# Convolution diagonals of a second Mamba block made early and kept in DRAM, spare TensorE products at the start, and two blocks of softplus sums on GpSimd

## The chip, the cores and the metric

The kernel runs on one core of one Trainium2 chip, in one launch. The metric is the device time of an execution in microseconds (us). The engines are called as in the profile: PE is TensorE (PEld its weight loads), DVE is VectorE, ACT is ScalarE, POOL is GpSimd, SP is SyncE, whose queue only issues DMAs.

## The reference, cut to what matters

The network has four layers. The change touches the first alone, a group normalization of the input (2 images, 256 channels, 32 x 32 pixels) followed by two Mamba blocks:

```
def mamba_block(x, ...):                      # x: 2 x 1024 tokens x 256 channels
    xs, res = split(u @ in_w + in_b)          # 512 channels each
    xs = silu(depthwise_conv4(xs, conv_w) + conv_b)
    dt, Bm, Cm = split(xs @ xproj_w)          # 16, 16 and 16 columns
    delta = softplus(dt @ dt_w + dt_b)
    dA  = exp(delta * -exp(A_log))            # 16 states for each channel
    dBu = delta * Bm * xs
    h_t = dA_t * h_(t-1) + dBu_t              # a scan over the tokens of an image
    y   = sum_n(h * Cm) + xs * D
    return (y * silu(res)) @ out_w + out_b

xt = xt + layernorm(mamba_block(xt, m1...))
xt = flip(xt); xt = xt + layernorm(mamba_block(xt, m2...)); xt = flip(xt)
```

Behind it come an attention over shifted pixels, a linear attention with a mixture of experts, and a softmax attention with a second mixture of experts. All is in float32.

## The kernel before

Channels lie on the 128 partitions, in four blocks (`dc` = 0 to 3) of the 512 inner channels; tokens lie along the free dimension, in chunks of 512. There are four chunks, two to an image, so that layer 0 has eight units: block m1 with chunks 0 to 3, then m2 with chunks 0 to 3. Each chunk goes through four generators of class `Mamba`.

- `enter` (L337) projects the chunk (`in_w`) into `pre`, which has three more columns ahead for the convolution; they are set to zero on POOL for an image's first chunk and copied from the chunk before otherwise.
- `front` (L360) makes all that the scan needs. The convolution of length 4 is four TensorE products per block with diagonal weights `taps[:, dc * 4 + k, :]` (L383): 128 x 128 matrices that hold 128 convolution weights on their diagonal. Then come the silu, the product with `xproj_w` (L405), which gives `xd`, and the softplus. The latter is computed as max(v, 0) + ln(1 + exp(-|v|)): `project` takes the absolute value (L446) and the positive part (L448 or L450), `powers` takes the exponential and the logarithm and w (L455 to L464), and `sums` (L467) makes four additions and products out of these, the last of which is `du` = delta * xs.
- `scan` (L498) is the scan of one unit. For each of the 16 states n it loads row n of B for all partitions (`m_b`, SP queue, four buffers), multiplies `du` with it in two halves of 128 x 1024 (`m_h<-m_du,m_b`, six buffers), lets ACT make exp(delta * A) for each block (L569) and DVE scan along 512 tokens (L573): 64 scans a unit. `rest` turns the states to token-major on PE (L527, L529) and weighs them with C, on ACT for five states and on DVE for the others (L543).
- `back` (L593) gates, projects out, normalizes and adds. It takes the term xs * D as a TensorE product with four further diagonals, `skip` (L632).

The first chunk has no scan of another to lie beside, and so has a `front` of its own (`alone=True`): its convolution runs on PE for blocks 0 and 2 and as four tap steps each on DVE for blocks 1 and 3 (L370, L375); DVE takes the positive part (L448) and w (L460) of all four blocks; the four sums of each block are on DVE; and DVE multiplies both halves of the first state (L557).

The order of the work is set in four ways. Layer 0 is laid out by `layer0` (L718): `paced` (L695) spreads the steps of the next chunk's `front` and of the last chunk's `back` over the 63 slots between the scans of a unit, by the slots given in `steps`. POOL's instructions go through `net.lined` (L174), which holds each one behind the one before it in the program. `tc.issue_after(i)` holds an instruction behind i. Beyond that the framework plans the order on each engine when it compiles, and the trace shows places where it isn't that of the source: some products of the second image's normalization (L248) stand between those of the first chunk's projection (L353).

The lines that matter for the change are these. `GroupNorm.image` (L238) normalizes one image: statistics on DVE, two small products on PE (L248, L257), the root on ACT (L159, L160) and four steps on DVE (L263). `diagonals` (L305) makes the 16 matrices of `taps` on POOL, each as identity times a column. It is called at once for m1, and for m2 at L784, as 16 steps over slots 24 to 40 of unit 2. `load_rest` (L316) loads the gate's and the output's weights and makes the four `skip` matrices on POOL, for m1 at once, for m2 in unit 4, the second part at slot 62. `load` (L292) makes `aneg` = -exp(A_log), on ACT (L301) and DVE (L302). Each of `taps` and `skip` has one buffer, which m2 takes over from m1. `delta` and `du` have two buffers each.

Of the kernel before, what the change touches and what calls it, by code (L numbers as in the profile page):

```python
# [10 lines left out]
F32 = mybir.dt.float32  # L11
# [8 lines left out]
P = 128  # L20
# [7 lines left out]
TC = 512  # L28
# [3 lines left out]
NDC = DI // P  # L32
# [186 lines left out]
class GroupNorm:  # L219
# [3 lines left out]
    def __init__(self, net, pool, psum, x):  # L223
# [12 lines left out]
        )  # L236

    def image(self, b):  # L238
        net, nc, pool, x = self.net, self.net.nc, self.pool, self.x
        n = NCC  # L240
        mv = pool.tile([P, n, 2], F32, name=f"gn_mv{b}")
        for cc in range(NCC):
            st = net.small.tile([P, 2, 6], F32, tag="gn_st", name=f"gn_st{b}{cc}")
            for h in range(2):
                nc.vector.bn_stats(out=st[:, h, :], in_=x[:, cc, b, h * 512 : (h + 1) * 512])
            nc.vector.bn_aggr(out=mv[:, cc, :], in_=st.rearrange("p h s -> p (h s)"))
        ps = self.psum.tile([P, TC], F32, tag="ht", name=f"gn_ps{b}")
        nc.tensor.matmul(ps[:, :n], lhsT=self.grp, rhs=mv[:, :, 0], start=True, stop=True)  # L248
        gm = pool.tile([P, n], F32, name=f"gn_gm{b}")
        nc.vector.tensor_copy(gm, ps[:, :n])  # L250

        d = pool.tile([P, n], F32, name=f"gn_d{b}")
        nc.vector.tensor_sub(d, mv[:, :, 0], gm)
        nc.vector.tensor_mul(d, d, d)
        nc.vector.tensor_add(d, d, mv[:, :, 1])
        ps = self.psum.tile([P, TC], F32, tag="ht", name=f"gn_ps2{b}")
        nc.tensor.matmul(ps[:, :n], lhsT=self.grp, rhs=d, start=True, stop=True)  # L257
        rs = pool.tile([P, n], F32, name=f"gn_rs{b}")
        net.rstd(rs, ps[:, :n])
        for h in range(2):  # L260
            for cc in range(NCC):
                xh = x[:, cc, b, h * TC : (h + 1) * TC]
                nc.vector.tensor_scalar(  # L263
                    xh, xh, gm[:, cc : cc + 1], rs[:, cc : cc + 1], ALU.subtract, ALU.mult
                )


class Mamba:
# [11 lines left out]
    def __init__(self, net, m, pools, xt, x, in_w, out_w, xproj_w, dt_w):  # L280
        self.net, self.m, self.xt, self.x = net, m, xt, x
        self.wpool, self.one, self.two, self.scanp, self.dram, self.ps_mm, self.ps_da, self.ps_ht = pools
        self.weights = in_w, out_w, xproj_w, dt_w
        self.chunks = {}
        self.due, self.pre = {}, {}

# [17 lines left out]

    def diagonals(self):  # L305

        self.taps = self.wpool.tile(
            [P, NDC * 4, P], F32, tag="taps", name=f"{self.m}_taps"
        )
        for i in range(NDC * 4):  # L310
            self.net.lined(
                self.net.nc.gpsimd.tensor_scalar_mul, self.taps[:, i, :], self.net.ident, self.net.col(f"{self.m}_conv_w", i)
            )
            yield

    def load_rest(self):  # L316

        net, nc, m, wpool = self.net, self.net.nc, self.m, self.wpool
        in_w, out_w, xproj_w, dt_w = self.weights
        self.gate_sb = wpool.tile([P, NCC, DI], F32, tag="gate_w", name=f"{m}_gate_sb")  # L320
        nc.sync.dma_start(self.gate_sb, in_w[:, :, DI:])
        yield
        self.out_sb = wpool.tile([P, NDC, C], F32, tag="out_w", name=f"{m}_out_sb")
        nc.sync.dma_start(self.out_sb, out_w)

        self.skip = wpool.tile([P, NDC, P], F32, tag="skip", name=f"{m}_skip")
        for dc in range(NDC):
            net.lined(
                nc.gpsimd.tensor_scalar_mul, self.skip[:, dc, :], net.ident, net.col(f"{m}_D", dc)
            )  # L330
        yield
# [4 lines left out]

    def enter(self, j):  # L337

        net, nc, m, one = self.net, self.net.nc, self.m, self.one
        tok = slice(j * TC, (j + 1) * TC)  # L340
        if not self.first(j):
            carry = self.wpool.tile([P, NDC, 3], F32, tag="carry", name=f"{m}_carry_{j}", bufs=2)
            net.lined(nc.gpsimd.tensor_copy, carry, self.entered[:, :, TC : TC + 3])
        self.entered = pre = one.tile([P, NDC, 3 + TC], F32, tag="pre", name=f"{m}_pre_{j}")
        self.pre[j] = pre
        if self.first(j):
            net.lined(nc.gpsimd.memset, pre[:, :, 0:3], 0.0)
        else:
            net.lined(nc.gpsimd.tensor_copy, pre[:, :, 0:3], carry)
        for mc in range(NDC):  # L350
            ps = self.ps_mm.tile([P, TC], F32, tag="mm", name=f"{m}_in_{j}_{mc}")
            for kc in range(NCC):
                nc.tensor.matmul(  # L353
                    ps, lhsT=self.in_sb[:, kc, mc * P : (mc + 1) * P], rhs=self.xt[:, kc, tok],
                    start=(kc == 0), stop=(kc == NCC - 1),
                )
            nc.scalar.activation(pre[:, mc, 3:], ps, AF.Identity, bias=net.col(f"{m}_in_b", mc))
            yield

    def front(self, j, alone=False):  # L360

        net, nc, m, one, two = self.net, self.net.nc, self.m, self.one, self.two
        eng = nc.vector if alone else nc.gpsimd
        pre = self.pre.pop(j)
        xs = two.tile([P, NDC, TC], F32, tag="xs", name=f"{m}_xs_{j}", bufs=3)
        silus = []
        for dc in range(NDC):
            b = net.col(f"{m}_conv_b", dc)
            if alone and dc % 2:
# [4 lines left out]
                for k in range(1, 4):  # L374
                    nc.vector.scalar_tensor_tensor(  # L375
                        xs[:, dc, :], pre[:, dc, k : k + TC],
                        net.col(f"{m}_conv_w", dc * 4 + k), xs[:, dc, :], ALU.mult, ALU.add,
                    )
# [58 lines left out]
        def project(eb, a):  # L437
            for k, dc in enumerate(range(a.start, a.stop)):
# [7 lines left out]
                nc.scalar.activation(eb[:, k, :], ps, AF.Abs, bias=b)  # L446
                if alone:
                    nc.vector.tensor_scalar(delta[:, dc, :], ps, b, 0.0, ALU.add, ALU.max)  # L448
# [17 lines left out]

        def sums(eb, lb, w, a):  # L467
            d = delta[:, a, :]
# [10 lines left out]
        if alone:  # L479
            for a in parts:  # L480
                w = du[:, a, :]
                yield from project(e[:, a], a)
                yield from powers(e[:, a], ln[:, a], w)
                yield from sums(e[:, a], ln[:, a], w, a)
        else:
# [12 lines left out]
    def scan(self, j, before, between, start=False, last=False):  # L498
# [50 lines left out]
        for n in range(NS):  # L549
# [3 lines left out]
            for g in range(NDC // G):  # L553
                h = scanp.tile(half, F32, tag="h", name=f"{m}_h_{j}_{n}_{g}", bufs=6)
                factors = du[:, g * G : (g + 1) * G, :], b.unsqueeze(1).to_broadcast(half)
                if start and n == 0:
                    nc.vector.tensor_mul(h, *factors)  # L557
# [160 lines left out]
def layer0(net, x, x_dram, m1, m2, load_image, taps, conv_dram, lg):  # L718
# [5 lines left out]
    with (  # L724
# [17 lines left out]
        blocks[0].load()  # L742
        for _ in blocks[0].diagonals():
            pass
        load_image()
# [3 lines left out]
        for m, r in zip(blocks, rows):  # L749
            m.out_b = r  # L750
        norm.image(0)

        units = [(m, j) for m in blocks for j in range(NCH)]
        norm.image(1)
        for _ in chain(units[0][0].enter(0), units[0][0].front(0, alone=True)):
            pass
        before, done, late = iter(()), [], []
        aside = taps.make(ps_mm, conv_dram)
        for u, (m, j) in enumerate(units):
# [1489 lines left out]
```

## Time and profile before

| | us |
|---|---|
| median of 3 runs | 2053.76 (2052.34 to 2054.6) |
| the profiled execution | 2042.13 |
| its span, first to last instruction | 2040.4 |
| layer 0 before its first scan | 50.5 |
| units 0 to 7, first scan to first scan | 113.4, 115.4, 122.7, 117.5, 119.6, 115.9, 119.4, 137.5 |
| busy in the whole span: PE, DVE, ACT, POOL | 1863.5, 1336.7, 947.2, 1062.2 |

How to read the profile: a line of a timeline has the start in us from the beginning of the span, the length in us, the engine (a q behind it is the engine's queue, which only issues), the line of the kernel, the operation, what is written and what is read, the shapes and the number of instructions merged into the line; in brackets behind it stand the idle time of the engine before it and who ended that. A line of a table of stretches has the stretch, its length, busy time and number of instructions for each engine, the granted share of the TensorE clock, and the share and rate of the DMA engines. L179 is the line of the helper `lined`, under which all of POOL's instructions of layer 0 appear; they are told apart by what they write. `m_taps` and `m_skip` are diagonals, `m_h` the products of `du` and B, `m_du`, `m_e` and `m_delta` the sums of the softplus.

### The profile page before, as it was taken

The page shows a single profiled execution, that of the slowest core. Times are in us where ns is not written, and L with a number is a line of the kernel's source. Part 1 is how long each engine was busy: PE and PEld are TensorE (multiplying, and loading weights), DVE is VectorE, ACT ScalarE, POOL GpSimd, SP SyncE. Part 2 cuts the span into 40 slices and gives each one's busy share as a digit, 9 for nine tenths or more (in the row PEclk, how much of TensorE's full clock was granted, in tenths as well). Part 3 has the DMA queues.
Part 4 walks back from the last instruction along what each step waited for, and adds up shares of the span by engine and source line. Part 5 has one row for each costly group of instructions (what it writes and reads, how often), then busy time and mean ns, then how long its engine had stood idle before and what let it go on. Part 6 is the DMA issues. An engine that isn't in the chain of part 4 may idle for free. (4 is left out here: it accounts for less than half of the span.)

```text
span 2040.4 us, 27838 instructions
## 1 busy us (share of the span) xinstructions
PE 1863.5 (91%) x9924; PEld 1336.6 (66%) x9924; DVE 1336.7 (66%) x2145; ACT 947.2 (46%) x1712; POOL 1062.2 (52%) x721
## 2 busy tenths in 40 slices
PE   7888987988898888899999989999999899999995
PEld 3465664656555565655566555568999666799994
DVE  6889899899988988898614285774222445652223
ACT  4787876777877777774302253332111122221111
POOL 3788898988979798994504260012333200023331
PEclk9789998999999999899999999999999999999997
DMA  3334354253435434362130100056999400358995
GB/s 125 98 91 118 86 123 107 70 132 85 128 90 117 108 76 123 78 146 67 31 58 1 52 0 1 24 196 247 322 324 324 183 21 21 142 179 319 329 333 201
DMA packets 98344, 269.15 MB, mean 132 GB/s; under 512 B 35851, under 2 KB 54160, under 8 KB 82068
## 3 DMA queue, kind: packets, MB, share of 16 engines
q1 hardware_dynamic: 80980, 196.72, 29.2%
q0 software_dynamic: 14208, 67.00, 13.5%
q10 hardware_dynamic: 3008, 3.55, 0.5%
q8 instruction: 83, 1.36, 0.3%
q14 instruction: 65, 0.53, 0.1%
HBM read 199.48 MB, written 21.46 MB: 108 GB/s over the span
## 5 line engine op out<-in xcount | busy, mean ns | idle before, releaser
L179 POOL TENSOR_TENSOR m_h<-m_du,m_b 128x1024 f32<-128x1024 f32 x254 | 604.6, 2470 | 160.0 <-PE m_ht L529 61.2
L569 ACT ACTIVATE m_da<-m_delta,m_aneg 128x512 f32<-128x512 f32 x512 | 349.6, 694 | 153.7 <-DVE m_h L573 150.7
L573 DVE TENSOR_TENSOR_SCAN m_h<-m_da,m_state,m_h 128x512 f32<-128x512 f32 x256 | 314.4, 1268 | 24.7 <-POOL m_h L179 15.1
L529 PEld LDWEIGHTS m_ht<-ident,m_h 128*128 128x128 f32 x1600 | 195.5, 148 | 198.1 <-issue 70.0
L529 PE MATMUL m_ht<-ident,m_h 128*128 128x128 f32 x1600 | 259.0, 289 | 60.8 <-DVE m_ya L543 30.1
L573 DVE TENSOR_TENSOR_SCAN m_h<-m_da,m_h 128x512 f32<-128x512 f32 x256 | 299.9, 1208 | 18.5 <-ACT m_da L569 11.7
L543 DVE SCALAR_TENSOR_TENSOR m_ya<-m_ht,m_ct,m_ya 128x512 f32<-128x512 f32 x324 | 231.9, 735 | 59.2 <-PE m_ht L529 53.1
L2008 PEld LDWEIGHTS h<-xts,we_l_late 128*128 128x128 f32 x2048 | 238.3, 192 | 9.1 <-issue 4.3
L2008 PE MATMUL h<-xts,we_l_late 128*128 128x128 f32 x2048 | 239.7, 275 | 4.4 <-DMA we_l_late<-in_l_experts_dram 2.9
L2016 DVE TENSOR_TENSOR hid<-hid,h 128x512 f32<-128x512 f32 x79 | 54.3, 687 | 233.9 <-PE h L2008 229.9
L1747 POOL DMA_INDIRECT x_l_early<-l_zs,l_source x15 | 17.4, 1158 | 340.5 <-ACT pt L1511 138.3
L2015 ACT ACTIVATE hid<-h 128x512 f32<-128x512 f32 x79 | 47.2, 597 | 315.4 <-issue 241.0
L527 PE MATMUL m_ht<-ident,m_h 128*128 128x128 f32 x896 | 137.0, 299 | 26.6 <-ACT m_s L541 9.4
L527 PEld LDWEIGHTS m_ht<-ident,m_h 128*128 128x128 f32 x896 | 120.1, 205 | 50.7 <-DVE m_h L573 17.6
L1747 POOL DMA_INDIRECT x_l_late<-l_zd,source x64 | 65.5, 1024 | 147.4 <-PE xt L1991 144.4
L2023 PE MATMUL o<-we_l_late,hid 128*128 128x256 f32 x512 | 122.7, 381 | 4.1 <-DVE y L2028 2.8
L383 PE MATMUL m_conv<-m_pre,m_taps 128*128 128x512 f32 x240 | 119.1, 615 | 4.1 <-ACT m_xs L389 4.1
L2030 POOL DMA_INDIRECT l_yd<-y,target x64 | 65.5, 1023 | 104.5 <-DVE y L2028 92.1
L541 ACT ACTIVATE m_s<-m_ht,m_ct 128x512 f32<-128x512 f32 x156 | 104.5, 686 | 27.8 <-PE m_ht L527 12.0
L2023 PEld LDWEIGHTS o<-we_l_late,hid 128*128 128x128 f32 x512 | 91.8, 190 | 15.3 <-DVE y L2028 3.9
L942 PE MATMUL early_acc<-x,early 128*98 128x448 f32 (+24 forms) x308 | 98.6, 446 | 0.4 <-DVE lg L959 0.4
L942 PE MATMUL acc<-x,pair 128*98 128x416 f32 (+21 forms) x308 | 93.3, 450 | 0.0
(399 smaller groups left out, 3104.3 us busy)
## 6 DMA issues: line engine op xcount, KB each, us to landing
we_l_late<-in_l_experts_dram SPq DMA_DIRECT2D x64, 1536.0 KB
m_yb<-m_s POOLq DMA_DIRECT2D x39, 1024.0 KB
m_b<-m_bd SPq DMA_DIRECT2D x128, 256.0 KB
we_l_early<-in_l_experts_dram SPq DMA_DIRECT2D x15, 1536.0 KB
m_ya<-m_yb POOLq DMA_DIRECT2D x7, 1024.0 KB
w<-in_l_w_dram SPq DMA_DIRECT2D x21, 256.0 KB
l_yl<-l_yd SPq DMA_DIRECT2D x8, 512.0 KB
l_zd<-l_z SPq DMA_DIRECT2D x7, 512.0 KB
```

Source lines behind the costliest of these rows:

```text
L179: self.line = do(*args, **named)
L383: nc.tensor.matmul(ps, lhsT=self.taps[:, dc * 4 + k, :], rhs=pre[:, dc, k : k + TC], start=(k == 0), stop=(k == 3),)
L527: nc.tensor.matmul(a, lhsT=h, rhs=net.ident, start=True, stop=True)
L529: nc.tensor.transpose(a, h, net.ident)
L541: nc.scalar.activation(to[:, i, :], ps, AF.Copy, scale=c)
L543: nc.vector.scalar_tensor_tensor(ya[:, i, :], ps, c, ya[:, i, :], ALU.mult, ALU.add)
L569: net.decayed = nc.scalar.activation(da, delta[:, dc, :], AF.Exp, scale=self.aneg[:, i : i + 1])
L573: nc.vector.tensor_tensor_scan(h, da, h, 0.0 if first else state[:, n, dc : dc + 1], ALU.mult, ALU.add)
L942: nc.tensor.matmul(a[:, lo - 16 * k : hi - 16 * k, co : co + n], lhsT=lhsT, rhs=self.x[:, kc, b, lo - r0 : hi - r0, ci : ci + n], start=(u ...
L1747: nc.gpsimd.indirect_dma_start(out=x, out_offset=None, in_=rows[:, :], in_offset=bass.IndirectOffsetOnAxis(ap=source[:, g : g + 1], axis=0 ...
L2008: nc.tensor.matmul(ps[:, at], lhsT=w12[:, s, kc, at], rhs=xt[:, kc * P : (kc + 1) * P], start=(kc == 0), stop=(kc == NCC - 1),)
L2023: gate.o = nc.tensor.matmul(ps[:, :C], lhsT=ht[:, mc * P : (mc + 1) * P], rhs=w[:, 8 + mc, :], start=(mc == 0), stop=(mc == NHC - 1),)
```

## The change

- **The diagonals of m2.** `keep_diagonals` makes all 20 of them on POOL right behind the first chunk's projection in the program, in buffers borrowed from the pools of `delta` and `du`, and writes them to DRAM by two DMAs from POOL's queue. The steps on POOL in unit 2 are gone; at slot 34 of that unit one DMA on SP fetches the 16 matrices of `taps` into their buffer. `load_rest` of m2 fetches `skip` in the same way.
- **Spare products.** `warm` issues products on PE whose result nobody reads: two of 512 columns ahead of the first image's first small product, two of 128 columns behind it, and three of 128 columns behind the second small product.
- **The second image's normalization** is cut in two. The first part, with the statistics and the small products, is held behind the first image's last normalization step and the third block's projection of the first chunk; the second part, with the root and the four steps on the image, behind the last tap step on DVE and the return of the exponential's table on ACT.
- **The first chunk.** The zero columns of `pre` are set on DVE. The positive part of block 3 goes from DVE to ACT. The sums of blocks 2 and 3 go from DVE to POOL (outside of `lined`). DVE multiplies three halves of states, not two: both of the first state and one of the second.

```diff
+    def warm(self, rows, n, *after):
+        net = self.net
+        ps = self.psum.tile([P, TC], F32, tag="ht", name="warm")
+        with ExitStack() as order:
+            for i in after:
+                order.enter_context(net.tc.issue_after(i.ins))
+            for _ in range(n):
+                net.nc.tensor.matmul(
+                    ps[:, : rows.shape[1]], lhsT=net.ident, rhs=rows, start=True, stop=True
+                )
...
+        if b == 0:
+            self.warm(x[:, 0, b, :TC], 2)
         ps = self.psum.tile([P, TC], F32, tag="ht", name=f"gn_ps{b}")
-        nc.tensor.matmul(ps[:, :n], lhsT=self.grp, rhs=mv[:, :, 0], start=True, stop=True)
+        last = nc.tensor.matmul(ps[:, :n], lhsT=self.grp, rhs=mv[:, :, 0], start=True, stop=True)
+        if b == 0:
+            self.warm(net.ident, 2, last)
...
+        last = nc.tensor.matmul(ps[:, :n], lhsT=self.grp, rhs=d, start=True, stop=True)
+        if b == 0:
+            self.warm(net.ident, 3, last)
+        yield
         rs = pool.tile([P, n], F32, name=f"gn_rs{b}")
         net.rstd(rs, ps[:, :n])
...
+    def scaled(self, out, name):
+        for i in range(out.shape[1]):
+            self.net.lined(
+                self.net.nc.gpsimd.tensor_scalar_mul, out[:, i, :], self.net.ident, self.net.col(name, i)
+            )
...
+    def keep_diagonals(self):
+        net, nc, m = self.net, self.net.nc, self.m
+        self.kept = []
+        for tag, name, n in (("delta", f"{m}_conv_w", NDC * 4), ("du", f"{m}_D", NDC)):
+            room = self.two.tile([P, NDC * 4, P], F32, tag=tag, name=f"{name}_room")[:, :n, :]
+            self.scaled(room, name)
+            kept = self.dram.tile([P, n, P], F32, tag=f"kept_{tag}", name=f"{name}_kept", bufs=1)
+            net.lined(nc.gpsimd.dma_start, kept, room)
+            self.kept.append(kept)
+
+    def fetch_diagonals(self):
+        self.net.nc.sync.dma_start(self.taps_tile(), self.kept[0])
+        yield
...
-        self.skip = wpool.tile([P, NDC, P], F32, tag="skip", name=f"{m}_skip")
-        for dc in range(NDC):
-            net.lined(
-                nc.gpsimd.tensor_scalar_mul, self.skip[:, dc, :], net.ident, net.col(f"{m}_D", dc)
-            )
+        if self.kept:
+            nc.sync.dma_start(self.skip_tile(), self.kept[1])
+        else:
+            self.scaled(self.skip_tile(), f"{m}_D")
         yield
...
-        if self.first(j):
+        if alone:
+            nc.vector.memset(pre[:, :, 0:3], 0.0)
+        elif self.first(j):
             net.lined(nc.gpsimd.memset, pre[:, :, 0:3], 0.0)
...
-        eng = nc.vector if alone else nc.gpsimd
...
-                if alone:
+                if alone and dc < 3:
                     nc.vector.tensor_scalar(delta[:, dc, :], ps, b, 0.0, ALU.add, ALU.max)
                 else:
                     nc.scalar.activation(delta[:, dc, :], ps, AF.Relu, bias=b)
...
-        def sums(eb, lb, w, a):
+        def sums(eb, lb, w, a, eng=nc.gpsimd):
...
-                yield from sums(e[:, a], ln[:, a], w, a)
+                eng = nc.vector if a.start < 2 else nc.gpsimd
+                yield from sums(e[:, a], ln[:, a], w, a, eng)
...
-                if start and n == 0:
+                if start and 2 * n + g < 3:
                     nc.vector.tensor_mul(h, *factors)
...
-        norm.image(0)
+        for _ in norm.image(0):
+            pass
         units = [(m, j) for m in blocks for j in range(NCH)]
-        norm.image(1)
-        for _ in chain(units[0][0].enter(0), units[0][0].front(0, alone=True)):
+        for _ in units[0][0].enter(0, alone=True):
+            pass
+        blocks[1].keep_diagonals()
+        opening = units[0][0].front(0, alone=True)
+        second = norm.image(1)
+        with tc.issue_after(norm.normed.ins), tc.issue_after(units[0][0].projected.ins):
+            next(second)
+        for _ in islice(opening, 5):
+            pass
+        with tc.issue_after(units[0][0].weighed.ins), tc.issue_after(net.loaded.ins):
+            for _ in second:
+                pass
+        for _ in opening:
             pass
...
-                steps.append((blocks[1].diagonals(), NDC * 4, 24, 40))
+                steps.append((blocks[1].fetch_diagonals(), 1, 34, 35))
```

More of the change, by code (lines that the diff above doesn't have):

```diff
@@ L256, in image @@
         ps = self.psum.tile([P, TC], F32, tag="ht", name=f"gn_ps2{b}")
-        nc.tensor.matmul(ps[:, :n], lhsT=self.grp, rhs=d, start=True, stop=True)
+        last = nc.tensor.matmul(ps[:, :n], lhsT=self.grp, rhs=d, start=True, stop=True)
+        if b == 0:
+            self.warm(net.ident, 3, last)
+        yield
         rs = pool.tile([P, n], F32, name=f"gn_rs{b}")
@@ L262, in image @@
                 xh = x[:, cc, b, h * TC : (h + 1) * TC]
-                nc.vector.tensor_scalar(
+                self.normed = nc.vector.tensor_scalar(
                     xh, xh, gm[:, cc : cc + 1], rs[:, cc : cc + 1], ALU.subtract, ALU.mult
@@ L284, in __init__ @@
         self.chunks = {}
-        self.due, self.pre = {}, {}
+        self.due, self.pre, self.kept = {}, {}, []
     def load_in(self):
@@ L303, in load, with taps_tile @@
         self.state = wpool.tile([P, NS, NDC], F32, tag="state", name=f"{m}_state", bufs=2)
-    def diagonals(self):
+    def scaled(self, out, name):
[3 more added lines that the diff above has]
+            )
+    def taps_tile(self):
         self.taps = self.wpool.tile(
@@ L309, in diagonals, with skip_tile @@
         )
-        for i in range(NDC * 4):
-            self.net.lined(
-                self.net.nc.gpsimd.tensor_scalar_mul, self.taps[:, i, :], self.net.ident, self.net.col(f"{self.m}_conv_w", i)
-            )
-            yield
+        return self.taps
+    def skip_tile(self):
+        self.skip = self.wpool.tile([P, NDC, P], F32, tag="skip", name=f"{self.m}_skip")
+        return self.skip
+    def diagonals(self):
+        self.scaled(self.taps_tile(), f"{self.m}_conv_w")
+    def keep_diagonals(self):
[10 more added lines that the diff above has]
+        yield
     def load_rest(self):
@@ L324, in load_rest @@
         nc.sync.dma_start(self.out_sb, out_w)
-        self.skip = wpool.tile([P, NDC, P], F32, tag="skip", name=f"{m}_skip")
-        for dc in range(NDC):
-            net.lined(
-                nc.gpsimd.tensor_scalar_mul, self.skip[:, dc, :], net.ident, net.col(f"{m}_D", dc)
-            )
+        if self.kept:
+            nc.sync.dma_start(self.skip_tile(), self.kept[1])
+        else:
+            self.scaled(self.skip_tile(), f"{m}_D")
         yield
@@ L335, in first, with enter @@
         return j % (HW // TC) == 0
-    def enter(self, j):
+    def enter(self, j, alone=False):
         net, nc, m, one = self.net, self.net.nc, self.m, self.one
@@ L352, in enter @@
             for kc in range(NCC):
-                nc.tensor.matmul(
+                product = nc.tensor.matmul(
                     ps, lhsT=self.in_sb[:, kc, mc * P : (mc + 1) * P], rhs=self.xt[:, kc, tok],
@@ L356, in enter @@
                 )
+            if mc == 2:
+                self.projected = product
             nc.scalar.activation(pre[:, mc, 3:], ps, AF.Identity, bias=net.col(f"{m}_in_b", mc))
@@ L374, in front @@
                 for k in range(1, 4):
-                    nc.vector.scalar_tensor_tensor(
+                    self.weighed = nc.vector.scalar_tensor_tensor(
                         xs[:, dc, :], pre[:, dc, k : k + TC],
@@ L742, in layer0 @@
         blocks[0].load()
-        for _ in blocks[0].diagonals():
-            pass
+        blocks[0].diagonals()
         load_image()
```

## The prediction

> **What bounds the kernel now.** All the code that changes lies in layer 0, so I first asked for busy time over the eight scan units (a unit is one chunk of 512 tokens, from its first scan to the next unit's). Columns: length, then busy time of PE, weight loads, DVE, ACT and POOL.
>
> ```profile
> 163.92:279.31 115.39, 102.95 (x535) 69.20 (x535) 107.39 (x119) 89.33 (x138) 98.37 (x49) 0.97 0.41 104
> 279.31:401.99 122.68, 103.67 (x537) 68.70 (x535) 109.89 (x120) 93.06 (x171) 109.67 (x66) 0.96 0.42 105
> 519.49:639.11 119.62, 106.94 (x551) 71.18 (x552) 104.33 (x118) 93.93 (x174) 102.71 (x54) 0.97 0.44 110
> ```
>
> DVE is busiest in all three (93%, 90%, 87%). Unit 2 (second line), which builds the second block's 16 diagonals on POOL, is the longest of the first seven, though POOL is full in it only with their help. So I looked for the place, counting scans in the DVE timeline: unit 2 reaches its scan 32 after 55.87 us and unit 4 after 55.22; scan 36 after 66.99 and 60.95; the last, 63, after 121.06 and 115.66. All of the 5.4 us is lost around scan 36. There the DVE timeline and the POOL timeline show:
>
> ```profile
> 337.55 3.44 DVE L573 TENSOR_TENSOR_SCAN m_h<-m_da,m_h 128x512 f32<-128x512 f32 x3
> 340.91 5.53 DVE L302 TENSOR_SCALAR m_aneg<-m_aneg 128x64 f32<-128x64 f32 x1
> 346.30 3.44 DVE L573 TENSOR_TENSOR_SCAN m_h<-m_da,m_h 128x512 f32<-128x512 f32 x3
> ```
>
> ```profile
> 340.43 1.27 POOL L179 TENSOR_SCALAR m_taps<-ident,cols_sb 128x128 f32<-128x128 f32 x2
> 341.58 4.73 POOL L179 TENSOR_TENSOR m_h<-m_du,m_b 128x1024 f32<-128x1024 f32 x2
> ```
>
> L302 took 0.28 us at the start of the program. Here it lasts until POOL's run of diagonals and products ends, and DVE's queue stands behind it. From 324 to 341 us DVE runs without a gap although POOL makes diagonals, so their 10 us cost nothing there; what costs is that they let POOL run unbroken into the products.
>
> The four diagonals of `m2_D` stand at the end of unit 4, again in the POOL timeline and then DVE's:
>
> ```profile
> 634.40 2.36 POOL L179 TENSOR_SCALAR m_skip<-ident,cols_sb 128x128 f32<-128x128 f32 x4
> 636.74 4.65 POOL L179 TENSOR_TENSOR m_h<-m_du,m_b 128x1024 f32<-128x1024 f32 x2
> ```
>
> ```profile
> 639.11 1.28 DVE L573 TENSOR_TENSOR_SCAN m_h<-m_da,m_state,m_h 128x512 f32<-128x512 f32 x1 [2.77 <-POOL m_h L179]
> ```
>
> The same boundary, unit 2 to 3, has 0.42 us of this wait. Last, the start. PE is the chain from 11.92 to 31.84 us, then ACT and DVE make the softplus, and DVE's sums hold back the scans:
>
> ```profile
> 48.81 1.21 DVE L557 TENSOR_TENSOR m_h<-m_du,m_b 128x1024 f32<-128x1024 f32 x1
> ...
> 50.54 1.21 DVE L573 TENSOR_TENSOR_SCAN m_h<-m_da,m_h 128x512 f32<-128x512 f32 x1
> ...
> 53.39 2.46 DVE L557 TENSOR_TENSOR m_h<-m_du,m_b 128x1024 f32<-128x1024 f32 x1
> 55.78 2.33 DVE L573 TENSOR_TENSOR_SCAN m_h<-m_da,m_h 128x512 f32<-128x512 f32 x2
> ```
>
> **What the Trainium skill says.** "SBUF — State Buffer", section "Who interferes with whom": DVE and GpSimd share a port pair under an exclusive lock; a DVE instruction in a two-port mode, or with two SBUF inputs against a GpSimd one that reads SBUF, waits for it whole. The trace agrees: 5.53 us against 0.28, and the 2.46 us product above against 1.21 free. "TensorE: Matmul & The Clock Gate", section "What's actually happening": TensorE starts at half clock and is released after some 3.4 us of work. The trace agrees: from 11.92 us weight loads follow one another each 0.85 us, from 15.44 us each 0.43.
>
> **The change, part by part.** Durations are of the profiled execution (2042.13 us, span 2040.4).
>
> Unit 2 loses 16 diagonals of 0.64 us, 10.3 us of POOL, which lie beside DVE's work. Gained is only what L302 loses less. POOL then works 4.68 of each 7.75 us (four scans of 1.21 and four L543 of 0.73 a state), so L302 meets a pair with chance 0.6 and then waits half of it, 2.35: 1.4 us expected. Gain 5.4 − 1.4 = 4.0; bounds 0 (caught whole again) and 5.4. The fetch that replaces them is one 1 MB DMA on SP. It waits for the last L383 of block 1 (317.6 us), with the loads of `b` queued behind it, and POOL waits for those; four `b` buffers hold three states, over 20 us, and the fetch's slot comes nine slots after the convolution's last: nothing. Its data is needed first at 403 us.
>
> Unit 4 loses four diagonals, 2.36 us, all in POOL's unbroken run in front of the product that DVE waits for: 2.77 falls to 0.4. Gain 2.3 (2.0 to 2.4). A 256 KB fetch takes their place, hidden.
>
> The start, first TensorE. The spare products (2 of 512 columns, 5 of 128) keep it working from about 5.5 us, when DVE's first statistics show that `x` is there. A product is two records in the trace (8 of `enter`'s products are 16 matmuls), and four of these then take 0.43 in place of 0.85: 1.7 gained. But the two wide products at half clock, 4 × 0.85 = 3.4, end at 8.9, and the first GroupNorm product started at 8.53: 0.4 lost. Net 1.3; 0.4 lost if the clock isn't released.
>
> POOL now makes 20 diagonals from 18.1 us, where it was idle until 42.87: 20 × 0.62 and two DMA issues of 0.87 (the later `m_yb` row), 14 us, so until 32. Behind them in POOL's line stand only the two `carry` copies (22.20 and 28.41 us), for a convolution at 46.8. The kept 1 MB, at the 404 GB/s that the loads reached between 8.9 and 12.3 us, takes 2.6 us and is out before the loads of `b` at 34.1; the `delta` and `du` buffers lent to it are wanted again in the middle of unit 0. All this is covered, except for the port: eight DVE tap steps (L370, L375) from 18 to 26 us have SBUF inputs and meet them. A wait between nothing and one diagonal, 0.62: I take half, 8 × 0.3 = 2.4. DVE ended at 25.6; the last silu, 0.63, and the table load, 1.28, then end at 30.0, and `xd` would be ready at about 30.5. So the slack takes nearly all; I charge 0.4. The second image's statistics now wait for the third projection (about 16.5 us), with tap steps queued behind them on DVE, and its normalization for the last tap step; both stay beside PE's chain: nothing, and if that slack is gone, the normalization's four steps of 0.48 us. The memset of `pre` on DVE is 0.1 us, before its first tap step.
>
> The softplus: DVE loses eight sums of 0.68 and one L448 of 0.75, and gains a product of 1.21: 5 us less. (ACT takes the L448 of block 3 as one step of 0.68, wanted only by POOL's seventh sum: nothing.) But the second product needs `du` of blocks 2 and 3, now from POOL. POOL begins when w of block 2 is there (42.2 before, 41.3 with the 0.9 gained), makes eight steps of 1.27 (the 128x512 additions of L691 in POOL's rows), 10.2 us, and loses perhaps 0.6 to DVE's steps: 52.1. Its own next product, 2.4, likely takes the port first: 54.5; then DVE's product, 1.2: scans go on at 55.7 against 55.78. In the hole before it DVE can do the third product and up to two scans of the second state, 2.4 us; I take half. Together the start gives 0.1 + 1.2 = 1.3. Its bounds are rivals B and C: 6 gained, 8.8 lost.
>
> Sum: 4.0 + 2.3 + 1.3 = 7.6. Behind layer 0 nothing changes and each layer waits for the one before, so it comes through whole: 2042.1 − 7.6 = 2034.5 for the profiled execution. The median of the runs, 2053.76, lies 11.6 above that execution; I take the same saving from it: **2046.2**.
>
> **The rivals.**
> A, the diagonals were hidden all along: L302 lands behind a pair again and the start is a draw. Then only unit 4 remains: 2053.76 − 2.3 = 2051.5. For it: DVE had no gap beside the diagonals. Against it: unit 4 does without the stall.
> B, the start opens wide: POOL's sums begin at 37.5 us, when the exponential of block 2 is there, and both scans go ahead: 6 us, and L302 slips through, 5.4. 2053.76 − 13.7 = 2040.1. Against it: DVE made that w only at 41.8.
> C, slower: the port. At L302 DVE got in neither between diagonals nor between products. If each of eight tap steps waits for two diagonals, 1.24, they end at 35.5 and the table load at 37.4, where `xd` was copied at 31.88: 5.5 later. POOL's sums then begin at 42.2 + 5.5 = 47.7 and, each behind a DVE step of 0.69, take 10.2 + 5.5; with both products scans go on at 67.0, 11.2 later, less 2.4 for the two early ones: 8.8 lost, and L302 is caught again. 2053.76 + 8.8 − 2.3 = 2060.3. It decides from a wait of 0.9 a tap step: 25.6 + 7.2 + 1.9 = 34.7 is 2.8 later than 31.88, which less the 0.4 of the softplus is as much as unit 4 gains. Against it: four L263 steps took 2.11 us beside diagonals and 1.91 without.
> That the spare products don't raise the clock is inside the forecast's range: 1.7 less.
>
> **How the numbers follow.** A measurement of this kernel can tell about 0.2%, 4.1 us, from no change. Chances: forecast 0.52, A 0.20, B 0.16, C 0.12. The forecast's own range is 2041.5 to 2049.5, which lies below 2049.65, the bound of faster; with B that is 0.68. A is no change; with C's milder part 0.22. Slower 0.10. The range reaches over A and B and leaves out C and the ends: 2038 to 2053.
>
> **What would show it.** In the trace of the changed kernel: no taps on POOL in unit 2, and its length near 118.5; L302 short, or long with 4.7 us of POOL products beside it (then A). At the boundary of units 4 and 5 a wait of about 0.4 for POOL. Weight loads of `enter` each 0.43 us from the first on. Scan 2 of unit 0 near 55.7, or with C tap steps of over 1.3 us. I am wrong at the root if units without diagonals (1, 3, 5) change by more than 2 us each, since then the order of instructions has moved elsewhere.

## The result and the profile after

| | before | changed |
|---|---|---|
| median of 16 runs each, us | 2052.22 | 2045.97 |
| lowest and highest | 2049.23, 2057.59 | 2036.73, 2052.41 |
| ratio, 95% interval | | 0.9967 (0.9953 to 0.9980) |
| the profiled execution; its span | 2042.13; 2040.4 | 2050.42; 2048.7 |
| first scan, scan 8 of unit 0, end of the last scan | 50.54, 62.87, 1011.9 | 42.67, 63.66, 1014.3 |
| units 0 to 7 | 113.4, 115.4, 122.7, 117.5, 119.6, 115.9, 119.4, 137.5 | 122.9, 116.6, 117.7, 117.5, 119.1, 116.4, 124.1, 137.5 |

The changed kernel is 0.33% faster, 6.3 us between the medians. The forecast was 2046.2, or 7.6 us less. But the one execution that was profiled took 8.3 us *longer* than the one profiled before the change. Executions of one kernel differ by as much (8.4 us between the lowest and highest of the kernel before, 15.7 of the changed one), so the two traces can't be subtracted as wholes; they can be read place by place. The stretches of units 1, 2, 4 and 6 of the changed kernel (length, busy time of PE, weight loads, DVE, ACT, POOL, then the granted TensorE clock):

```profile
165.52:282.15 116.63, 102.93 (x528) 69.74 (x526) 108.03 (x119) 88.78 (x138) 99.57 (x49) 0.96 0.41 103
...
282.15:399.83 117.68, 104.19 (x541) 69.48 (x542) 105.86 (x120) 93.48 (x172) 98.92 (x50) 0.97 0.44 118
...
517.29:636.37 119.08, 105.69 (x538) 70.97 (x538) 106.47 (x119) 92.77 (x170) 102.12 (x50) 0.96 0.44 113
...
752.73:876.81 124.08, 107.54 (x492) 69.54 (x492) 106.43 (x120) 87.28 (x158) 110.79 (x56) 0.89 0.46 107
```

Unit 2 has lost 16 instructions and 10.8 us on POOL and is 5.0 us shorter. Unit 4 is only 0.5 us shorter. Unit 6, which the change doesn't touch, is 4.7 us longer at a granted clock of 0.89, where it had 0.93.

**Unit 2.** L302 is now L321. DVE's timeline and POOL's:

```profile
342.37 1.74 DVE L321 TENSOR_SCALAR m_aneg<-m_aneg 128x64 f32<-128x64 f32 x1
```

```profile
341.70 4.66 POOL L179 TENSOR_TENSOR m_h<-m_du,m_b 128x1024 f32<-128x1024 f32 x2 [3.65 <-ACT m_da L617]
```

It still runs into a pair of POOL's products, but only until about the end of the first of them (341.70 + half of 4.66 = 344.03; it ends at 344.11): 1.74 us for 5.53. Unit 2 reaches its scan 36 after 61.88 us, where it took 66.99. Of these 5.1 us, 3.7 lie between scans 32 and 36, where L302 stands. The other 1.4 were won ahead of scan 32, and the second trace of the kernel before, shown further below, has them too.

**The boundary of units 4 and 5.** In DVE's timeline the wait of 2.77 us for POOL is gone, but a small step of the layer normalization (128 x 4 elements, 0.16 us when nothing is in its way) now takes 2.36 us, beside a pair of POOL's products:

```profile
625.11 2.36 DVE L200 TENSOR_TENSOR ln_off<-ln_off,ln_rs 128x4 f32<-128x4 f32 x1
...
634.12 2.34 DVE L621 TENSOR_TENSOR_SCAN m_h<-m_da,m_h 128x512 f32<-128x512 f32 x2 [0.67 <-ACT m_da L617]
636.37 1.26 DVE L621 TENSOR_TENSOR_SCAN m_h<-m_da,m_state,m_h 128x512 f32<-128x512 f32 x1
```

```profile
622.78 4.67 POOL L179 TENSOR_TENSOR m_h<-m_du,m_b 128x1024 f32<-128x1024 f32 x2
```

**The start.** Weight loads of the first projection are 0.43 us apart from its second on, and `xd` is copied at 30.19 us, 1.69 earlier:

```profile
11.93 0.30 PEld L399 LDWEIGHTS m_in<-x,m_in_sb 128*128 128x128 f32 x2 [0.63 <-DVE x L282]
12.47 0.19 PEld L399 LDWEIGHTS m_in<-x,m_in_sb 128*128 128x128 f32 x1 [0.24 <-DVE x L282]
12.90 0.19 PEld L399 LDWEIGHTS m_in<-x,m_in_sb 128*128 128x128 f32 x1 [0.24 <-issue]
```

The first scans start at 42.67, 7.9 us earlier. Then DVE stands still until POOL has made the last `du`, and the gain is gone:

```profile
42.67 2.34 DVE L621 TENSOR_TENSOR_SCAN m_h<-m_da,m_h 128x512 f32<-128x512 f32 x2
52.52 4.50 DVE L605 TENSOR_TENSOR m_h<-m_du,m_b 128x1024 f32<-128x1024 f32 x2 [7.52 <-POOL m_du L521]
56.95 7.90 DVE L621 TENSOR_TENSOR_SCAN m_h<-m_da,m_h 128x512 f32<-128x512 f32 x7
```

```profile
40.58 3.11 POOL L521 TENSOR_TENSOR m_du<-m_e,m_du 128x512 f32<-128x512 f32 x1 [5.38 <-DVE m_du L507]
...
51.22 1.27 POOL L521 TENSOR_TENSOR m_du<-m_delta,m_xs 128x512 f32<-128x512 f32 x1
52.57 8.97 POOL L179 TENSOR_TENSOR m_h<-m_du,m_b 128x1024 f32<-128x1024 f32 x3
```

So the earlier first scan is no gain by itself: scan 2 starts at 56.95 (55.78 before) and scan 8 at 63.66 (62.87).

### The profile page after: what moved, and what is told of

Its sections match the earlier page's. It is cut to its first block, busy times and chain, and to the rows that moved or that the text cites. A ratio compares the mean times of both kernels' runs of the same rounds, so it can differ in the third digit from the quotient of the medians.

```text
span 2048.7 us, 27882 instructions
## 1 busy us (share of the span) xinstructions
PE 1874.6 (92%) x9938; PEld 1344.7 (66%) x9938; DVE 1332.1 (65%) x2138; ACT 946.9 (46%) x1713; POOL 1074.4 (52%) x729
## 5 line engine op out<-in xcount | busy, mean ns | idle before, releaser
L575 PEld LDWEIGHTS m_ht<-ident,m_h 128*128 128x128 f32 x896 | 124.3, 212 | 52.5 <-DVE m_h L621 16.8
L2082 PE MATMUL o<-we_l_late,hid 128*128 128x256 f32 x512 | 122.7, 381 | 4.1 <-DVE y L2087 2.8
L430 PE MATMUL m_conv<-m_pre,m_taps 128*128 128x512 f32 x240 | 117.7, 609 | 5.8 <-ACT m_xs L436 3.4
```

What stands on the lines that cost most here:

```text
L430: nc.tensor.matmul(ps, lhsT=self.taps[:, dc * 4 + k, :], rhs=pre[:, dc, k : k + TC], start=(k == 0), stop=(k == 3),)
L575: nc.tensor.matmul(a, lhsT=h, rhs=net.ident, start=True, stop=True)
L2082: gate.o = nc.tensor.matmul(ps[:, :C], lhsT=ht[:, mc * P : (mc + 1) * P], rhs=w[:, 8 + mc, :], start=(mc == 0), stop=(mc == NHC - 1),)
```

## The experiments

Two theories stood against each other at first. One: the kept diagonals bring the gain, through L302, and the start brings nothing. The other: the gain comes from the start, and what unit 2 wins is lost elsewhere. Later runs ask which part of the start works against it, and what a better version is. Ratios are to the kernel before.

**Kept diagonals alone** (the kernel before with `keep_diagonals`, `fetch_diagonals` and the fetch of `skip`, nothing else of the change).

```diff
-        for _ in chain(units[0][0].enter(0), units[0][0].front(0, alone=True)):
+        for _ in units[0][0].enter(0):
+            pass
+        blocks[1].keep_diagonals()
+        for _ in units[0][0].front(0, alone=True):
...
-                steps.append((blocks[1].diagonals(), NDC * 4, 24, 40))
+                steps.append((blocks[1].fetch_diagonals(), 1, 34, 35))
```

> Of the change only the kept diagonals; the start is as before, and the 20 diagonals follow the first projection on POOL. Theory (the diagonals paid for themselves, the start gave nothing): unit 2 falls from 122.7 to about 117.5 us, the wait for POOL at the boundary of units 4 and 5 from 2.8 to 0.4, and the time by 7 us, ratio 0.9965. Rival (the gain came from the start, the diagonals were hidden): unit 2 stays within 1 us of 122, ratio 0.999 to 1.001. Third (port): the tap steps of the first chunk wait for the new diagonals, first scan over 1 us later than 50.5.

Measured: 0.9970 (0.9956 to 0.9984), median 2047.13; scan 8 of unit 0 at 63.88 us, unit 2 117.7, unit 4 115.6. In DVE's timeline:

```profile
341.79 1.76 DVE L302 TENSOR_SCALAR m_aneg<-m_aneg 128x64 f32<-128x64 f32 x1
...
622.86 0.15 DVE L200 TENSOR_TENSOR ln_off<-ln_off,ln_rs 128x4 f32<-128x4 f32 x1
...
632.41 1.28 DVE L598 TENSOR_TENSOR_SCAN m_h<-m_da,m_state,m_h 128x512 f32<-128x512 f32 x1 [0.41 <-POOL m_h L179]
```

The kept diagonals alone have as much as the whole change. Here both gains that the forecast named are seen at their places: L302 in 1.76 us, and the boundary's wait in 0.41. L200 isn't caught (0.15 us). Of the 4.0 us by which unit 4 is shorter, the boundary's wait gives 2.4. The other 1.6 lie between its scans 40 and 44, where TensorE was at half clock for 3.41 us and not for 6.83, and DVE waited that much less for it. One expectation was not about the gain: a first scan over 1 us later than 50.5 was to show that the tap steps wait for the new diagonals. It came at 51.55. But the tap steps took 0.1 us longer at most; TensorE was at half clock to 17.30 us, where it had left it at 15.37, and its chain made `xd` 1.0 us later.

**The start alone** (the changed kernel without `keep_diagonals`; m2's diagonals on POOL in units 2 and 4 again).

```diff
-        blocks[1].keep_diagonals()
...
-                steps.append((blocks[1].fetch_diagonals(), 1, 34, 35))
+                steps.append((blocks[1].stepped(), NDC * 4, 24, 40))
```

> All of the change but the kept diagonals: the second block's 16 are made on POOL in unit 2 and its four in unit 4, as before. Theory: the first scan comes at 42.7 us, but scan 2 of unit 0 at about 57 against 55.8 before, unit 2 lasts 122 again, and the time is that of before, 0 to 1.5 us more, ratio 1.000. Rival (the start gives the gain): 5 to 7 us less, ratio 0.997.

Measured: 1.0007 (0.9992 to 1.0021), median 2056.35; scan 8 at 63.48, unit 2 121.9. The stall is back in its old form:

```profile
343.68 5.47 DVE L321 TENSOR_SCALAR m_aneg<-m_aneg 128x64 f32<-128x64 f32 x1
```

All the edits at the start together are worth nothing that can be measured. The second theory falls.

**L302 on ACT** (the kernel before with this one line changed; all diagonals stay on POOL in units 2 and 4).

```diff
-        nc.vector.tensor_scalar_mul(self.aneg, self.aneg, -1.0)
+        nc.scalar.activation(self.aneg, self.aneg, AF.Copy, scale=-1.0)
```

> The kernel before with the sign of aneg taken on ACT and not on DVE (L302); all diagonals stay where they were. Theory (in unit 2 only L302's wait for POOL's instructions costs): scan 36 of unit 2 comes at 61.5 us of the unit and not at 67.0, unit 2 lasts 117.5, and the time is 5 us less, ratio 0.9975. Rival (the 10 us of diagonals on POOL hold the products back): unit 2 keeps at least 121 us.

Measured: 0.9972 (0.9957 to 0.9987), median 2046.09. Unit 2:

```profile
278.00:391.66 113.66, 103.31 (x550) 69.61 (x550) 104.89 (x119) 93.07 (x173) 107.19 (x65) 0.99 0.45 113
```

POOL still has its 16 diagonals (65 instructions, 107 us) and the unit is 9 us shorter than before. Of that, 5.4 lie between scans 32 and 36, where L302 stood (5.73 us in place of 11.12), and 2.8 between scans 36 and 44. There TensorE was at half clock for 10.24 us before, right behind the stall, and not at all here, and DVE's waits for it fell from 3.57 to 0.93. These 2.8 us can't be booked as the edit's gain: units 1 and 3 of this execution were 2.6 and 3.7 us longer than in the first trace before. One moved instruction of 0.28 us thus brings as much as 20 matrices kept in DRAM, within the intervals: the 16 diagonals of unit 2 cost nothing that can be measured, only L302 behind them did. The four of unit 4 do cost: the boundary's wait is still 2.58 us here.

**One block's sums on POOL in place of two** (the changed kernel with block 2's sums on DVE).

```diff
-                eng = nc.vector if a.start < 2 else nc.gpsimd
+                eng = nc.vector if a.start < 3 else nc.gpsimd
```

> The changed kernel with the sums of block 3 alone on POOL; those of block 2 are on DVE. Theory (the scans wait for eight sums in a row on POOL, 52.5 us, and then for POOL's own product): four sums end near 48, DVE has no hole of 7.5 us, scan 2 of unit 0 comes at 52.5 to 55 us and not at 57.0, and the time is 2 to 4 us below the changed kernel's, ratio to before 0.995 to 0.996. Rival (DVE's own work sets the start): scan 2 at 57 or later.

Measured: 0.9947 (0.9931 to 0.9963), median 2042.52; scan 8 at 61.11, 2.6 us earlier than in the changed kernel, and scan 2 at 54.37, as expected. The interval overlaps that of the changed kernel.

**No spare products** (the changed kernel without the three calls of `warm`).

```diff
-        if b == 0:
-            self.warm(x[:, 0, b, :TC], 2)
...
-            self.warm(net.ident, 2, last)
...
-            self.warm(net.ident, 3, last)
```

> The changed kernel without the spare products. Theory (they keep TensorE at full clock from the first projection on): the first four weight loads of the projection follow each other by 0.85 us again and not by 0.43, xd is copied about 1.7 us later than 30.2, first scan at 44.4, scan 2 of unit 0 at 58.7, the time 1 to 2 us above the changed kernel's. Rival (POOL's sums set the start, so an earlier xd is worth nothing): scan 2 stays at 57.0 within 0.5 us.

Measured: 0.9974 (0.9962 to 0.9985), median 2048.02; `xd` at 32.90 and scan 8 at 66.37, both 2.7 us later than with them, where 1.7 was expected. Weight loads are 0.85 us apart up to 17.2 us:

```profile
16.34 0.33 PEld L393 LDWEIGHTS m_in<-x,m_in_sb 128*128 128x128 f32 x1 [0.52 <-issue]
17.20 0.33 PEld L393 LDWEIGHTS m_in<-x,m_in_sb 128*128 128x128 f32 x1 [0.52 <-issue]
17.82 0.19 PEld L393 LDWEIGHTS m_in<-x,m_in_sb 128*128 128x128 f32 x1 [0.29 <-issue]
```

The gain is plain in the trace; this interval and the changed kernel's overlap, so the times alone don't show it. How large it is depends on when TensorE leaves half clock without spare products: 14.95 to 17.58 us in the five traces that have none.

**All sums on DVE** (the changed kernel; POOL has no sums at the start and gets back the third product).

```diff
-                eng = nc.vector if a.start < 2 else nc.gpsimd
+                eng = nc.vector
...
-                if start and 2 * n + g < 3:
+                if start and n == 0:
```

> The changed kernel with all four blocks' sums on DVE and only the first state's two products on DVE, as before. Theory: first scan near 48.5 us, scan 2 of unit 0 near 54 (55.8 before, less the 1.7 that the front gains), between the kernel with one block on POOL (52.9 at best) and the changed one (57.0); ratio to before 0.9955 to 0.996. Rival (GpSimd's share of the sums is what makes the start faster): scan 2 at 57 or later, ratio 0.998.

Measured: 0.9947 (0.9928 to 0.9967), median 2044.08. Scan 0 starts at 47.10, 4.4 us *later* than in the changed kernel, and scan 8 at 58.22, 5.4 us earlier. Without POOL's sums the start gives 4.7 us over the kernel before (58.22 against 62.87). The sums on POOL are what ate it.

**One block on POOL and L302 on ACT**, together.

```diff
-        nc.vector.tensor_scalar_mul(self.aneg, self.aneg, -1.0)
+        nc.scalar.activation(self.aneg, self.aneg, AF.Copy, scale=-1.0)
...
-                eng = nc.vector if a.start < 2 else nc.gpsimd
+                eng = nc.vector if a.start < 3 else nc.gpsimd
```

> One block's sums on POOL, and the sign of aneg taken on ACT, so that nothing of it waits for POOL. Theory: L302's remaining 1.76 us in unit 2 is gone, the time 1.5 us below the kernel with one block on POOL: ratio 0.994. Rival (what is taken off DVE there comes back at the next wait): ratio 0.9947 as without.

Measured: 0.9931 (0.9909 to 0.9953), median 2039.42. In the trace the stretch between scans 32 and 36 of unit 2 falls from 7.41 to 5.73 us; the interval overlaps that of the version without the second edit.

**The layer normalization's small steps on ACT as well** (the version above; L192 and L200, which took up to 2.4 us behind POOL, become five small ACT steps).

```diff
-            nc.vector.tensor_sub(off, self.zeros[:, :n], mv[:, :, 0])
...
-            nc.vector.tensor_mul(off, off, rs)
+            for i in range(n):
+                nc.scalar.activation(
+                    off[:, i : i + 1], mv[:, i, 0:1], AF.Copy, scale=rs[:, i : i + 1]
+                )
+            nc.scalar.activation(off, off, AF.Copy, scale=-1.0)
```

> As the last, and the two small products of each layer normalization with two operands in SBUF (L192 and L200, up to 2.3 us each beside POOL's products) are made on ACT in five small steps. Theory (they wait for POOL's port like L302): some 5 us of DVE time in layer 0 are freed, at least half of it seen in the time, ratio 0.992 to 0.9935. Rival (ACT's steps and the later start of its normalization eat it): ratio 0.994 or more.

Measured: 0.9963 (0.9949 to 0.9976), median 2047.12: a miss. DVE's waits over layer 0 (total, times, longest), first without and then with this edit:

```profile
DVE m_ya L591 <- PE m_ht L577: 50.9, 43, 5.0
...
DVE m_ya L591 <- PE m_ht L575: 7.5, 7, 4.3
DVE ln_off L200 <- ACT ln_rs L160: 4.5, 4, 2.3
```

```profile
DVE m_ya L594 <- PE m_ht L580: 55.7, 44, 5.2
...
DVE m_ya L594 <- PE m_ht L578: 19.4, 10, 4.1
```

Counting DVE's instructions of layer 0 that take over one and a half times the shortest of their form, what they take beyond it fell from 9.9 to 2.1 us, and the wait for L160 went too. But the waits for TensorE's turned states grew from 58.4 to 75.1 us. In this trace TensorE, not DVE, was late at those places. Layer 0 explains only part: it is 3.2 us longer than in the trace without the edit, and 4.0 us more lie behind it. Why isn't shown; TensorE was granted less in these executions (0.965 in the mean against 0.9675).

**All sums on DVE and L302 on ACT.**

```diff
-        nc.vector.tensor_scalar_mul(self.aneg, self.aneg, -1.0)
+        nc.scalar.activation(self.aneg, self.aneg, AF.Copy, scale=-1.0)
...
-                eng = nc.vector if a.start < 2 else nc.gpsimd
+                eng = nc.vector
...
-                if start and 2 * n + g < 3:
+                if start and n == 0:
```

> The changed kernel with all sums of the first chunk on DVE, two products of the first state on DVE, and the sign of aneg taken on ACT: the two finds together. Theory: scan 8 of unit 0 at 58.2 us as with the sums on DVE (63.7 in the changed kernel), L302's 1.76 us gone, the time 7 us below the changed kernel's; ratio to before 0.992 to 0.994, the lowest of all. Rival (what the start gains is lost again behind it): ratio 0.9947 or more.

Measured: 0.9926 (0.9907 to 0.9946), median 2037.48, the fastest of all, and the only one whose interval lies clear below that of the changed kernel (0.9953 to 0.9980), though it overlaps that of the version with one block on POOL. DVE at the start:

```profile
46.58 0.68 DVE L521 TENSOR_TENSOR m_du<-m_delta,m_xs 128x512 f32<-128x512 f32 x1
47.18 1.21 DVE L621 TENSOR_TENSOR_SCAN m_h<-m_da,m_h 128x512 f32<-128x512 f32 x1
48.31 2.25 DVE L605 TENSOR_TENSOR m_h<-m_du,m_b 128x1024 f32<-128x1024 f32 x1
50.48 9.06 DVE L621 TENSOR_TENSOR_SCAN m_h<-m_da,m_h 128x512 f32<-128x512 f32 x8
```

No hole: scan 2 is at 51.6 us and scan 8 at 58.32.

**Both kernels once more**, one execution each, to see what in the first pair of traces comes back. No edit.

> The changed kernel once more, for a second trace. If unit 6's wait of 4.4 us of DVE for PE comes from where TensorE's half-clock stretches fall in that execution, its length moves between 119 and 125 us; units 0 to 2 are within 1 us of the first trace, scan 8 of unit 0 at 63.7 within 1 us.

> The kernel before once more, for a second trace. Unit 2 lasts 122 us within 1.5 again, L302 in it 5.5 us, the boundary of units 4 and 5 has a wait of over 2 us for POOL; the span differs from the first trace's 2040.4 by up to 12 us, most of it behind layer 0.

Measured: spans of 2050.8 (changed) and 2055.4 (before); the last scan ends at 1012.4 and 1018.5. This pair differs by −6.1 us at the end of layer 0, the first by +2.4. L302 took 5.52 us before and 1.75 changed, and the boundary's wait before was 2.77 again. In the changed kernel L200 took 2.34 again and unit 4 was 119.1 long. Three expectations failed: the changed kernel's unit 0 differed by 1.9 us between its traces (1 allowed), the spans of the kernel before by 15.0 (12 allowed), and unit 6 of the changed kernel, which was to move if half-clock stretches of TensorE fall there as they will, came out at 124.1 again. It did move in the kernel before, from 119.4 to 121.6.

**The second product on POOL** (the changed kernel; DVE makes the first half of the first two states, and POOL the second half of the first, behind its sums).

```diff
-                if start and 2 * n + g < 3:
+                if start and n < 2 and g == 0:
```

> The changed kernel with the second half of the first state multiplied on POOL again, straight behind POOL's own sums, and DVE left with the first half of the first state and the first half of the second. Theory: in the changed kernel DVE's product of the second half, which stands first in DVE's queue, loses the port to POOL's next product and takes 3.4 us for 1.2, and the product of the second state stands behind it. With POOL making that half itself, DVE's product of the second state runs in the hole, scan 2 of unit 0 starts near 54.9 us where the changed kernel had 56.95, and scan 8 near 61.8 where it had 63.66. Rival: the eight sums on POOL set the time and it doesn't matter who makes the product behind them: scan 2 near 57 and scan 8 near 63.7. For the whole time both say less than 2 us of difference, which one look can't show; the trace is what tells them apart.

Measured: `xd` came 1.77 us later in this execution (31.96), as TensorE, though its spare products ran, fell back to half clock at 12.0 us:

```profile
12.49 0.34 PEld L399 LDWEIGHTS m_in<-x,m_in_sb 128*128 128x128 f32 x1 [0.48 <-DVE x L282]
...
15.66 0.19 PEld L399 LDWEIGHTS m_in<-x,m_in_sb 128*128 128x128 f32 x1 [0.27 <-issue]
```

So the places are read from `xd` on. Scan 2 comes 57.69 − 31.96 = 25.7 us behind it (26.8 in the changed kernel), scan 8 33.5 behind it (33.5). DVE's product is in the hole, as intended, but it takes the port from one of POOL's sums:

```profile
46.69 1.20 DVE L605 TENSOR_TENSOR m_h<-m_du,m_b 128x1024 f32<-128x1024 f32 x1
57.69 6.80 DVE L621 TENSOR_TENSOR_SCAN m_h<-m_da,m_h 128x512 f32<-128x512 f32 x6 [9.79 <-POOL m_h L179]
```

```profile
46.76 2.26 POOL L521 TENSOR_TENSOR m_du<-m_e,m_du 128x512 f32<-128x512 f32 x1
```

The port's share is real at scan 2 (1.0 of the 2.05 us expected) and nothing at scan 8. The rival holds there: POOL's run of eight sums and its next products sets the time. The expectation had one reading wrong: in the changed kernel the product of the second half took 1.23 us, and it was the third product, behind it, that took 3.36.

## Why the prediction came out as it did

**Unit 2: right.** Expected 4.0 us less, by L302 losing most of its 5.53. It lost 3.8, in both traces of the changed kernel; the unit's two traces before average 121.8 and the two after 117.7, 4.1 less. The view that the 10 us of diagonals are free and only the instruction caught behind them costs is shown by the run with L302 on ACT. Rival A falls in this part; its other half, that the start is a draw, came true. The Trainium skill ("SBUF — State Buffer", "Who interferes with whom") has whoever issues first holding the shared pair for a whole instruction; the 1.74 us agree with that, as L302 ended 0.05 us behind the first product. The 5.5 us, in three traces with diagonals in unit 2, are more than one instruction of POOL's, two diagonals and both products, and no run tells why DVE didn't get in between. That the size came out so well is partly luck. The forecast took L302's meeting with a pair as a draw and its 1.4 us as a mean over 0 and 2.35. It isn't a draw: in all seven traces with kept diagonals and L302 on DVE it starts 0.65 to 0.67 us into a pair and takes 1.74 to 1.76.

**Boundary of units 4 and 5: the stall went, the gain half came.** The wait for POOL fell from 2.77 to 0.41 with the kept diagonals alone and to none in the changed kernel. What the forecast lacked is what becomes late next. In the changed kernel's traces, L200 falls beside a pair of POOL's products 11 us ahead of the boundary and takes 2.36 and 2.34 us. The four scans around it (56 to 60) take 8.20 us for 5.94, so 2.2 of the 2.3 us go back. In three variants L200 escaped (0.14 or 0.15 us: no spare products, and the two with L302 on ACT that have one block's sums on POOL or none), and there unit 4 lasts 116.7 to 117.2, 2.4 to 2.9 less than before, which is the forecast's gain. That it is the same port was not tried alone for this place.

**The start: wrong, by 2.1 us.** Expected 1.3 less, measured 0.8 more at scan 8. Its terms:

- TensorE: `xd` 1.7 us earlier, 1.3 expected less 0.4 of slack. The spare products do what they are for, and the 0.4 that they were to cost isn't seen: the projection began at 11.93 us, against 11.92.
- The port at the tap steps, charged with a wait of 0.3 each: the six L422 took 0.752 us (median) beside POOL's diagonals, and 0.751 without. Rival C falls. The same section of the Trainium skill lets two SBUF inputs contend with a POOL instruction that reads SBUF; here DVE doesn't show it, and POOL does: its diagonals took 0.79 to 1.13 us beside the tap steps and 0.60 behind them.
- POOL's sums: begin expected at 41.3, end at 52.1; they began at 40.58 and ended at 52.5. Rival B falls.
- The step that failed is "up to two scans of the second state, 2.4 us; I take half". DVE's queue holds the product of the second half first, which needs POOL's last sum. The product that could have run, and the early scans, stand behind it: DVE did nothing for 7.52 us. The order at the port was wrong too: DVE's product of the second half came 0.05 us ahead of POOL's next and took 1.23, but the third product behind it met POOL's and took 3.36, and scan 2 stands behind both. So scan 2 came at 56.95, not 55.7. Together 1.2 + 1.25 = 2.4, about the miss.

The larger point was missed. The forecast asked when POOL's sums end, and found a draw with the kernel before, but not what DVE would do with them itself. Eight sums are 10 us on POOL and 5.4 on DVE, which stood idle for 7.5 us. With all of them on DVE scan 8 is 5.4 us earlier.

**The total** was close partly by luck. The start's 2 us too many and the boundary's lost 2 us would leave 3.3 of 7.6; measured are 6.8 (4.1 to 9.6; the ratio and its interval times 2052). Kept diagonals alone give 0.0030 × 2053.84 = 6.2 and the start alone −1.4, in sum 4.8; with intervals of some 3 us on each, the change as a whole agrees with that sum. A rest of some 3.5 us is not assigned to a place. Both traces of the changed kernel are of executions above its median, by 4.5 and 6.6 us, and the first trace before is of one 10.1 below, so what the traces show need not be what the middle execution does.

**Behind the start nothing changes: nearly so.** Units 1, 3 and 5 stayed within 1.3 us of the first trace. Unit 6 took 124.1 us in both traces of the changed kernel and 119.4 and 121.6 before. Most of it lies between its scans 48 and 52; here are the first trace before, the second, and the changed kernel:

```profile
843.49:852.38 8.89, 8.37 (x46) 6.65 (x46) 6.76 (x9) 8.89 (x16) 8.89 (x6) 1.00 0.30 69
843.63:856.11 12.48, 12.48 (x48) 9.30 (x47) 6.87 (x9) 9.34 (x16) 12.40 (x7) 0.67 0.35 77
841.02:853.70 12.68, 12.68 (x48) 9.44 (x47) 6.87 (x9) 9.34 (x16) 12.68 (x7) 0.66 0.49 108
```

DVE has nearly the same work in all three, and TensorE is busy throughout in the last two, at half clock for 10.24 us; DVE's waits for it are 5.2 to 5.5 us there in place of 1.8. Ten of the fourteen traces have this stretch of half clock, the second of the kernel before among them. Four don't, among them two variants with most of the change, the one with one block's sums on POOL and the one with the second product there; their unit 6 lasts 119.4. So the change is neither needed for it nor enough for it. What decides in which executions it falls there stays open.

## What to carry to other kernels

Ask of a stretch of helper work not what it costs but which instruction of the bottleneck engine is caught behind it: moving that one instruction of 0.28 us to an idle engine was worth as much as taking 20 matrices out of the way. When work goes to a slower engine to open the path, follow the receiver's whole queue to the moment when the giver needs the result, and look at what the giver does meanwhile: an earlier first scan was followed by a hole as long. And judge a change of 0.3% by medians, with single traces for places only; and before a difference at one place is booked to the change, see whether TensorE was at half clock there in one of the traces only.

## What the runs showed of the hardware

- Sums of 128 x 512 take 1.26 us on POOL and 0.68 on DVE, and products of 128 x 1024 2.34 and 1.2.
- A DVE product of 128 x 4 elements, 0.15 us when free, takes up to 2.36 beside POOL's products. The scans, which read one tensor in SBUF and one in PSUM (`m_da`), stay between 1.19 and 1.29 us in the changed kernel's whole layer 0.
- The spare products don't guarantee the clock. With them, `xd` came at 29.4 to 30.2 us in the other eight traces and at 31.96 in one, where TensorE fell back for 3.4 us. The Trainium skill ("TensorE: Matmul & The Clock Gate", "What's actually happening") says that the window that decides is free-running, so that the number of slow products varies from run to run; that fits, and isn't shown.
- The clock records of the fourteen traces have two shares, full and half. TensorE is at half clock for 124 to 169 us of the span, in stretches that are multiples of 3.41 us (but for the last, which the end of the span cuts): 137.5 in the first trace before, 158.0 in the first after.
- One such step more or less is seen in the time. Between scans 40 and 44 of unit 4, eleven traces have 6.83 us of half clock and take 12.41 to 12.48 us; the three that have 3.41 take 10.80 to 10.82.
- Single executions of a kernel spread over 8 to 22 us (2041.56 to 2063.18 in 75 of the kernel before). In the changed kernel the faster ones have the higher granted clock (0.969 at 2036.73 us, 0.962 at 2052.41, a correlation of −0.9 over its 16); in those 75 hardly so (0.967 at the lowest, 0.963 at the highest, and a correlation of −0.2).
